# Holding large loads to about two under way, each tied to a TensorE instruction, with new places for all work

## The chip, the cores and the metric

The kernel runs on one core of a Trainium2 chip. The core has five engines with a program each: TensorE (PE in the profile, with its weight loads shown apart as PEld), VectorE (DVE), ScalarE (ACT), GpSimd (POOL) and SyncE (SP). Here SP starts nearly all transfers between memory and the core. They are carried out by 16 DMA engines, which also bring the engines' programs. The metric is the device time of one execution in microseconds, lower is better.

## The reference

Two layers are applied to x, a float32 array of 8 sequences x 512 rows x 256 features.

```python
# layer 1: an expert per sequence
h = gelu(x @ Wi[e] + bi[e])                 # 256 -> 1024, exact gelu
r = h @ Wo[e] + bo[e] + x                   # 1024 -> 256
x = layernorm(r) * gamma[e] + beta[e]
# layer 2: attention with 16 heads of 16, and a feed-forward part
emb = silu(sin_cos(timestep)) @ W_ada + b_ada
scale, shift = split(emb)
x = layernorm(x) * (1 + scale) + shift
scores = q @ k.T / 4 + attention_bias       # 8 x 16 x 512 x 512
scores = where(mask, -inf, scores)
x = x + softmax(scores) @ v @ Wo + bo
x = x + gelu2(layernorm(x) * g2 + beta2, W1, b1) @ W2 + b2    # 256 -> 1024 -> 256
```

The attention bias, called fside, is 134 MB of the 192 MB that are read. It is used once, element by element.

## The kernel before

All eight sequences pass through three kinds of work, which the kernel lets overlap. The expert layer and the projections to q, k and v (matmuls of 128x128 blocks; lines 689, 712, 863 and 911), the attention, and the feed-forward part (lines 689, 712 again, and 1052 for the last sequence).

The attention goes in steps. A step takes 32 query rows of one sequence with all 16 heads. There are 16 steps for a sequence, 128 in all. `attention_step` (L1097) makes a step's operations: a load of 1 MB of fside (`load_f`, L1112), one of the mask for four steps (L1118), the mask's conversion on GpSimd (L1124), the score matmuls into four banks (L1147; in one step of four the mask is added there by a matmul, L1140), in the other three steps the addition of the mask to fside on GpSimd (L1162, four instructions), the addition of scores and fside with the row maximum on VectorE (L1170, four instructions), the maximum's sign on GpSimd (L1183), the exponentials on ScalarE (L1191) and the transposes on VectorE (L1206). The score matmuls of the next step wait for the four additions at L1170, since these empty the banks. After four steps `attend` (L1216) multiplies the probabilities with v (L1246, 512 matmuls in four groups called sums0 to sums3), brings the row sums into place (L1262), divides, and multiplies with the output weights (L1289).

The buffer for fside has five tiles of two steps each (L354): a tile is free for a new load when the sums of its four steps are done.

The order of the work is set by a planner that runs while the program is built. The class `Weave` (L143) collects operations with an engine, a cost, a key and what they depend on. `run` (L180) then walks through a model of time. It keeps for each engine when it is free. Again and again it takes the operation that can start first, and among those that can start within 0.25 us of it, the one with the lowest key; it emits that operation. The order on each engine is therefore fixed when the program is built, and each engine carries out its own list in that order. On the chip an engine waits for another only through semaphores.

The keys come from tables. `PLACES` gives for each sequence where the stretches of the expert layer, the projections, the values and the feed-forward part begin and end, in units of attention steps, and how far other engines are ahead (`place`, L1075). `DUE` gives the lead of each kind of operation of a step, `LAST_DUE` the same for the last four steps, `AHEAD` how long before its first use a weight or an x buffer is loaded, and `PUT_BACK` how much an operation is put back in the choice when it needs another ScalarE table or another form of TensorE's tiles.

The planner also models how TensorE gets its program. A program is read in packets of 256 words (an instruction is a word; a matmul with its weight load makes two). Packet k is asked for when TensorE comes to word 155 + 256k, and the words from 192 + 256(k+1) on need it (`ASKED`, `NEEDED`). A packet is taken to land 2.4 us after whatever loads stand in the queue are done, and no sooner than 3.4 us after the request.

Because loads can stand before a packet, the planner keeps large loads (0.3 MB or more) away from requests. If fewer than 100 words are left to the next request (`NEAR`), a large load is put off by 4 us. After a request a large load may start only 0.4 us later (`CLEAR`). To hold the chip to that, `behind` (L1327) adds a dependence: each large load waits for one TensorE operation, the first that in the plan ends 0.4 us or more after the latest request. All large loads up to the next request share it. How many loads are under way at once has no limit of its own; the model knows only the time at which the queue is done (`queue`, L265).

## Time and profile before

| | us |
|---|---|
| median of 3 runs | 903.15 (903.09 to 904.28) |
| profiled execution | 905.54 |
| its span, first to last instruction | 903.8 |

| engine | busy us | share of the span |
|---|---|---|
| TensorE matmuls | 883.8 | 98% |
| GpSimd | 747.6 | 83% |
| VectorE | 736.4 | 81% |
| ScalarE | 691.8 | 77% |
| 16 DMA engines, data | | 58.5% |

The granted TensorE clock is full over the whole span (mean 1.000). In a row of the profile's groups or waits, L and a number give the line of the kernel, `out<-in` the tiles written and read, and `<-` before another engine's name tells who ended a wait. A row of waits gives the microseconds in total, how often, and the longest. A row of the time line gives the start, the busy time and the instruction, with the idle time before it in square brackets. "issue" stands for time in which the engine waited for nothing that the profile shows. A matmul's end is modelled, so that overlapping matmuls can look longer than their pace.

### The profile page before, as it was taken

To read this page: it belongs to the slowest core of one execution; us is meant where nothing else is said; L and a number is where in the kernel's file an instruction comes from. 1 tells how busy PE (TensorE), PEld (TensorE's weight loads), DVE (VectorE), ACT (ScalarE), POOL (GpSimd) and SP (SyncE) were. 2 spreads that over 40 slices of the span, in tenths; PEclk is the share of its full clock that TensorE was granted. 3 is DMA by queue.
4 is the path that set the end of the run, shared out by engine and by line. 5 is a ranking of instruction groups with operands and counts; after the bars stand their busy time and mean duration, and the time that the engine had idled before them with its cause. 6 is when DMAs were issued, how large, how long until landed. Compare 5 with 4: busy or idle time off the path is not lost.

```text
span 903.8 us, 31828 instructions
## 1 busy us (share of the span) xinstructions
PE 883.8 (98%) x13073; PEld 521.6 (58%) x13073; DVE 736.4 (81%) x1715; ACT 691.8 (77%) x1525; POOL 747.6 (83%) x844
## 2 busy tenths in 40 slices
PE   6999999999999999999999999999999899999998
PEld 2664564654664656545656456465465465465687
DVE  1216989998898978999978999899999889989930
ACT  3147979859959876797786995987977968989743
POOL 1189989999998996999799998999998899988720
PEclk9999999999999999999999999999999999999999
DMA  7697175475487466575575766485753666366230
GB/s 235 207 419 272 60 262 194 162 268 214 168 281 296 152 268 227 190 270 208 210 301 180 279 246 239 173 314 175 285 215 138 245 256 260 154 264 240 107 108 24
DMA packets 43160, 197.99 MB, mean 219 GB/s; under 512 B 4772, under 2 KB 12278, under 8 KB 24582
## 3 DMA queue, kind: packets, MB, share of 16 engines
q1 hardware_dynamic: 42724, 195.91, 58.5%
q8 instruction: 102, 1.67, 0.8%
q14 instruction: 44, 0.36, 0.1%
q10 hardware_dynamic: 290, 0.04, 0.0%
HBM read 191.73 MB, written 4.21 MB: 217 GB/s over the span
## 4 chain that ended last, share of the span: by engine, by line
PE 69%; POOL 17%; DMA 6%; issue 3%; ACT 3%; DVE 1%; SPq 0%; POOLq 0%; ACTq 0%; DVEq 0%
PE d L712 20%; PE d L689 15%; PE sc L1147 10%; PE d L1246 10%; POOL fs L1162 9%; PE d L863 4%; DMA fs<-in_fside_Bx16xSxS_dram 4%; POOL xn L764 4%; PE d L1289 2%; PE d L911 2%; PE d L1052 2%; ACT fs L1191 1%; DMA xn<-in_x_dram 1%; POOL mh L1124 1%; PE d L667 1%
## 5 line engine op out<-in xcount | busy, mean ns | idle before, releaser
L1162 POOL TENSOR_TENSOR fs<-fs,mh 128x512 f32<-128x512 f32 x384 | 436.3, 1163 | 26.9 <-DMA fs<-in_fside_Bx16xSxS_dram 16.5
L1191 ACT ACTIVATE fs<-fs,top 128x512 f32<-128x512 f32 x512 | 363.8, 714 | 87.7 <-POOL top L1183 87.1
L1170 DVE CUSTOM_DVE_ANT_0 fs<-sc,fs 128x512 f32<-128x512 f32 x512 | 326.4, 683 | 54.0 <-POOL fs L1162 21.5
L1206 DVE STREAM_TRANSPOSE fs<-fs 128x1024 f32<-128x1024 f32 x256 | 305.9, 1220 | 4.0 <-ACT fs L1191 3.9
L712 PE MATMUL d<-w,hid 128*128 128x256 f32 x1024 | 239.4, 384 | 0.0
L689 PE MATMUL d<-xt,w 128*128 128x512 f32 x480 | 225.7, 610 | 9.8 <-DMA w<-in_L_cond_Wi_dram 6.8
L712 PEld LDWEIGHTS d<-w,hid 128*128 128x128 f32 x1024 | 189.6, 190 | 56.2 <-issue 27.9
L689 PEld LDWEIGHTS d<-xt,w 128*128 128x128 f32 x480 | 87.6, 192 | 126.8 <-issue 100.5
L1147 PE MATMUL sc<-k,q 32*64 32x512 f32 x2048 | 146.4, 606 | 0.0
L1246 PEld LDWEIGHTS d<-fs,vb 64*32 64x32 f32 x8192 | 113.3, 105 | 42.7 <-issue 31.6
L1246 PE MATMUL d<-fs,vb 64*32 64x128 f32 x8192 | 132.4, 272 | 1.3 <-issue 1.2
L1191 ACT ACTIVATION_READ_ACCUMULATOR fs<-fs,top 128x1 f32 x512 | 97.5, 191 | 0.0
L1124 POOL TENSOR_SCALAR mh<-m 128x512 bf16<-128x512 uint8 x128 | 79.7, 623 | 10.4
L794 ACT ACTIVATE hid<-d,bc 128x512 f32<-128x512 f32 x64 | 41.7, 686 | 36.0 <-PE d L689 33.0
L1147 PEld LDWEIGHTS sc<-k,q 32*64 32x64 f32 x2048 | 35.3, 130 | 52.6 <-issue 22.3
L730 DVE BATCH_NORM_STATS2 st<-xn 128x6 f32<-128x256 f32 x96 | 40.2, 419 | 13.3 <-POOL xn L764 11.0
L1191 ACT ACT_TABLE_LOAD x38 | 48.8, 1283 | 0.7
L764 POOL TENSOR_TENSOR xn<-xn,bo 128x1024 f32<-128x1024 f32 x8 | 18.9, 2363 | 36.5 <-DMA xn<-in_x_dram 22.7
L1183 POOL TENSOR_SCALAR top<-top 128x4 f32<-128x4 f32 x128 | 25.3, 198 | 24.4 <-DVE top L1170 14.6
L1170 DVE DVE_READ_ACCUMULATOR2_ANT top<- 128x1 f32 x512 | 42.9, 84 | 0.0
L764 POOL TENSOR_TENSOR xn<-xn,rows 128x1024 f32<-128x1024 f32 x16 | 38.0, 2372 | 4.3 <-ACT xn L743 3.5
L986 ACT ACTIVATE hid<-d,col 128x512 f32<-128x512 f32 x56 | 35.8, 686 | 7.2 <-PE d L689 6.8
(100 smaller groups left out, 750.5 us busy)
## 6 DMA issues: line engine op xcount, KB each, us to landing
fs<-in_fside_Bx16xSxS_dram SPq DMA_DIRECT2D x128, 1024.0 KB
w<-in_L_cond_W_dram SPq DMA_DIRECT2D x16, 1024.0 KB
w<-in_L_cond_Wo_dram SPq DMA_DIRECT2D x8, 1024.0 KB
m<-in_mask_Bx1xSxS_bk_dram SPq DMA_DIRECT2D x32, 256.0 KB
w<-in_L_cond_Wi_dram SPq DMA_DIRECT2D x7, 1024.0 KB
xt<-in_x_turned_dram SPq DMA_DIRECT2D x8, 512.0 KB
xn<-in_x_dram SPq DMA_DIRECT2D x8, 512.0 KB
out_dram<-xn SPq DMA_DIRECT2D x32, 128.0 KB
```

The lines of the kernel that those rows point to most:

```text
L689: nc.tensor.matmul(h.tile, wt[:, c, f * P : (f + 1) * P], src.tile[:, c, :], start=(c == 0), stop=(c == ND - 1),)
L712: nc.tensor.matmul(h.tile[:, :D], lhs(f), wt[:, f, :], start=(f == 0), stop=(f == n - 1))
L730: nc.vector.bn_stats(st, src[:, t, :])
L764: lambda: nc.gpsimd.tensor_tensor(xn[b].tile, xn[b].tile, tiled(row()), alu),
L794: lambda: nc.scalar.activation(hid.tile[:, f, :], h.tile, AF.Gelu, bias=bc[b].tile[:, f : f + 1]),
L1124: nc.gpsimd.tensor_scalar(mh.tile, m8.tile[:, s % NI, :].bitcast(U8), MASKED, 1.0, ALU.mult, ALU.mult)
L1147: nc.tensor.matmul(banks[u][64 * r : 64 * r + 64, :], q_h[b].tile[quads[u], r, i, :], k_h[b].tile[quads[u], r, :], start=not joins, stop=True,
L1162: nc.gpsimd.tensor_tensor(f()[:, u, :], f()[:, u, :], mh.tile, ALU.add)
L1170: nc.vector.tensor_tensor_reduce(out=f()[:, u, :], in0=banks[u], in1=f()[:, u, :], scale=1.0, scalar=-3.0e38, op0=ALU.add, op1=ALU.max, ac ...
L1191: nc.scalar.activation(f()[:, u, :], f()[:, u, :], AF.Exp, bias=top.tile[:, u : u + 1], accum_out=den.tile[:, u, s % NI : s % NI + 1],)
L1206: nc.vector.transpose(two, two)
L1246: nc.tensor.matmul(pc[r].tile[QB * u : QB * u + QB, :P], vb_h[b].tile[half, j, u, :], t[half, :, :, u, QB * j : QB * j + QB], start=(j == ...
```

## The change

Three things change. First, a large load may now start in the plan only when at most 4.2 us of earlier transfers are left in the queue (`APART`); at 0.37 MB per us this is about one and a half loads of 1 MB. Second, the time kept clear after a request for a packet goes from 0.4 to 1.0 us (`CLEAR`). Third, the dependence that holds a large load back is chosen anew for each load: `recent` keeps the TensorE operations in order, and the load is tied to the latest of them that in the plan ends no more than 0.4 us after the load's own start. The old tie was to the end of the request's surroundings, which could lie far before the load.

With these rules all numbers of `PLACES`, `DUE`, `LAST_DUE`, `PUT_BACK` and `AHEAD` are replaced. So the order of the work on every engine is another. The operations, their sizes and their count are the same. No function is added.

```diff
 PLACES = {
     "up": [
-        (-43.62, -35.76, -9.79), (-10.08, -7.54, -8.47), (4.82, 6.37, 0.8), (16.16, 24.72, 3.59),
-        (40.19, 40.49, 9.26), (58.26, 59.96, 10.32), (74.13, 78.66, 0.43), (95.87, 102.96, 10.54),
+        (-39.19, -21.79, 3.06), (-14.61, 8.16, 5.64), (8.37, 8.24, 8.25), (15.42, 18.73, 6.65),
+        (38.6, 37.95, 0.46), (59.2, 60.13, 11.84), (72.75, 77.81, 2.08), (96.93, 99.72, 10.87),
     ],
...
 DUE = {
-    "load_m": -2.8, "load_f": 0.36, "convert": 5.45, "add": 3.5, "neg": 1.21, "exp": 7.79,
+    "load_m": 6.41, "load_f": 5.61, "convert": 6.13, "add": 4.66, "neg": -2.34, "exp": 8.15,
...
 AHEAD = {
-    "xt": 4.43, "wi": 5.3, "br": 21.51, "x": 1.61, "wo": 0.08, "row": 6.69, "w1": -5.35,
-    "w2": -4.96, "ss": 4.57, "bo": 9.01,
+    "xt": 5.82, "wi": 5.25, "br": 41.81, "x": -2.64, "wo": 0.97, "row": 9.79, "w1": 1.45,
+    "w2": 1.17, "ss": 3.05, "bo": 23.49,
 }
...
-    CLEAR = 0.4
+    CLEAR, APART = 1.0, 4.2
...
-        queue, clear, gate, landed = 0.0, -100.0, None, 0.0
+        queue, clear, landed, recent = 0.0, -100.0, 0.0, []
...
                             else:
                                 start = max(start, clear)
+                            start = max(start, queue - self.APART)
...
-                    clear, gate = at + self.CLEAR, None
+                    clear = at + self.CLEAR
...
-            if o.words and clear > 0.0 and (gate is None or gate[0] < clear):
-                gate = o.end, behind(None)
-            elif o.mb >= self.LARGE and gate is not None:
-                behind(gate[1])
+            if o.words and clear > 0.0:
+                recent.append((o.end, behind(None)))
+            elif o.mb >= self.LARGE and recent:
+
+                while len(recent) > 1 and recent[1][0] <= start + 0.4:
+                    recent.pop(0)
+                behind(recent[0][1])
```

More of the change, by code (lines that the diff above doesn't have):

```diff
@@ L59 @@
     "up": [
-        (-43.62, -35.76, -9.79), (-10.08, -7.54, -8.47), (4.82, 6.37, 0.8), (16.16, 24.72, 3.59),
-        (40.19, 40.49, 9.26), (58.26, 59.96, 10.32), (74.13, 78.66, 0.43), (95.87, 102.96, 10.54),
+        (-39.19, -21.79, 3.06), (-14.61, 8.16, 5.64), (8.37, 8.24, 8.25), (15.42, 18.73, 6.65),
+        (38.6, 37.95, 0.46), (59.2, 60.13, 11.84), (72.75, 77.81, 2.08), (96.93, 99.72, 10.87),
     ],
     "down": [
-        (-11.81, -10.05, 10.14), (-4.58, 13.95, 4.54), (8.87, 9.47, -5.98), (16.73, 19.65, -6.3),
@@ L65 @@
-        (40.46, 45.48, -3.47), (63.1, 67.19, -0.71), (69.95, 82.78, -4.3), (102.74, 103.99, 6.51),
+        (-20.03, -11.72, -7.86), (-7.71, 12.63, -2.49), (6.73, 11.61, 1.05), (14.3, 20.63, -5.29),
+        (42.99, 49.92, 0.54), (61.05, 71.22, 1.14), (72.07, 81.04, -5.39), (105.02, 107.12, 5.37),
     ],
     "norm": [
-        (9.71, -15.53, 14.76), (31.23, 198.14, 17.88), (46.96, 90.03, 27.3),
-        (-3.29, 172.59, -35.11), (64, -55.76, 7.58), (21.93, 53.72, -44.84),
-        (100.13, -120.62, 10.02), (103.92, -117.57, -1.06),
+        (1.44, -38.7, 8.38), (26, 230.24, 14.14), (38.85, 67.91, 18.14), (-5.46, 108.96, -35.61),
@@ L71 @@
+        (66.49, -96.63, 12.39), (5.81, 47.02, -58.5), (102.37, -144.13, 12.92),
+        (103.33, -191.46, -0.18),
     ],
     "project": [
-        (-2.64, -1.11, -9.92), (20.49, 12.69, 2.54), (23.07, 26.86, -1.46), (36.89, 63.96, 2.72),
-        (53.64, 66.71, -4.18), (76.36, 89.67, -0.98), (90.61, 100.48, 0.78),
-        (102.39, 116.12, -9.49),
+        (-6.24, 4.45, -1.69), (14.02, 6.13, 1.1), (19.71, 44.68, 0.79), (32.51, 62.55, -4.48),
+        (58.72, 68.47, 5.17), (66.86, 87.88, 1.49), (87.82, 106.61, -1.02),
@@ L76 @@
+        (100.6, 111.25, -10.23),
     ],
     "values": [
-        (3.57, 9.1, -1), (21.82, 33.22, 1.13), (39.61, 33.8, 3.49), (53.58, 70.14, -0.86),
-        (69.81, 68.46, 2.46), (82.31, 97.69, -0.8), (101.06, 90.65, -0.17),
-        (112.56, 112.45, 0.87),
+        (6.85, -2.11, 4.05), (23.34, 28.83, 2.2), (41.39, 46.26, 5.73), (52.7, 76.41, 5.22),
+        (64.67, 74.8, -3.7), (87.1, 85.66, -1.39), (106.54, 94.05, 0.4), (120.74, 117.22, 0.29),
     ],
     "last_norm": [
-        (25.14, 12.56, 0.32), (40.69, 48.12, -3.3), (62.39, 53.06, -5.43), (81.92, 87.74, 3.92),
@@ L84 @@
-        (84.13, 103.16, 3.07), (109.67, 129.5, -5.33), (118.65, 123.92, -5.19),
+        (31.46, 14.48, 3.22), (47.66, 48.8, 3.82), (62.37, 45.5, 0.03), (87.36, 82.07, 9.04),
+        (80.56, 86.1, -12.16), (102.32, 101.81, -14.17), (113.14, 142.82, 1.95),
     ],
     "last_up": [
-        (28.82, 25.08, 6.08), (35.47, 40.18, 0.67), (66.32, 52.95, -1.98), (74.48, 89.37, -4.47),
-        (98.9, 107.27, -9.13), (112.96, 117.07, 1.01), (125.16, 123.41, 3.62),
+        (28.21, 27.9, -1.53), (45.03, 36.84, 0.32), (63.3, 61.62, -8.49), (78.86, 86.69, 1.7),
@@ L89 @@
+        (106.21, 105.05, -5), (115.6, 120.99, 3.41), (126.4, 122.67, 0.57),
     ],
     "last_down": [
-        (27.06, 36.61, -3.94), (55.01, 42.07, -1.93), (75.63, 60.54, 4.28), (81.96, 95.18, 4.08),
-        (104.06, 119.74, 1.18), (117.15, 124.04, 0.23), (125.29, 136.74, -0.43),
+        (33.42, 41.59, 2.09), (56.4, 48.61, -3.15), (70.03, 73.09, 6.84), (82.44, 89.88, 0.1),
+        (109.79, 121.46, -1.54), (127.98, 122, -1.76), (125.8, 143.77, 3.59),
     ],
     "last_part": [
-        (131.41, 259.4, -0.64), (259.56, 321.86, -1.29), (274.57, 311.97, 7.81),
+        (139.14, 253.36, 1), (286.03, 296.98, 0.82), (276.89, 303.93, -3.06),
@@ L99 @@
 DUE = {
-    "load_m": -2.8, "load_f": 0.36, "convert": 5.45, "add": 3.5, "neg": 1.21, "exp": 7.79,
-    "turn": 9.78, "rec": 11.99, "diagonal": 7.14, "sums0": 5.77, "sums1": 2.88, "sums2": 10.44,
-    "sums3": 4.92, "own": 7.36, "spread": 9.56, "divide": 7.43, "out": 10.17, "out_add": 12.64,
-    "load_f2": -1.03, "masked": 0.44,
+    "load_m": 6.41, "load_f": 5.61, "convert": 6.13, "add": 4.66, "neg": -2.34, "exp": 8.15,
+    "turn": 9.92, "rec": 11.1, "diagonal": 9.03, "sums0": 5.15, "sums1": 2.58, "sums2": 9.05,
+    "sums3": 3.42, "own": 5.11, "spread": 13.61, "divide": 8.42, "out": 10.91, "out_add": 14.5,
+    "load_f2": 5.25, "masked": -2.07,
 }
 LAST_DUE = {
-    "exp": 10.3, "turn": 1.32, "neg": -5.97, "rec": 16.75, "diagonal": 19.97, "sums0": 9.5,
-    "sums1": 3.93, "sums2": 10.9, "sums3": 19.76, "own": 12.05, "spread": 47.46, "divide": 57.23,
-    "out": 72.84, "out_add": 79.8,
+    "exp": 1.08, "turn": 8.34, "neg": 2.72, "rec": 31.77, "diagonal": 30.22, "sums0": 10.64,
+    "sums1": 13.03, "sums2": 17.16, "sums3": 20.95, "own": 31.22, "spread": 23.21,
+    "divide": 49.04, "out": 87.17, "out_add": 79.99,
 }
 PUT_BACK = {
-    "table": 12.31, "tiles": 0.6,
+    "table": 12.27, "tiles": 0.84,
 }
 AHEAD = {
-    "xt": 4.43, "wi": 5.3, "br": 21.51, "x": 1.61, "wo": 0.08, "row": 6.69, "w1": -5.35,
-    "w2": -4.96, "ss": 4.57, "bo": 9.01,
+    "xt": 5.82, "wi": 5.25, "br": 41.81, "x": -2.64, "wo": 0.97, "row": 9.79, "w1": 1.45,
+    "w2": 1.17, "ss": 3.05, "bo": 23.49,
 }
```

## The prediction

> **What bounds the kernel now.** I read the busy shares first, then TensorE's groups and waits, then the time line around its longest pause, and last the waits of the load queue and of GpSimd.

> ```profile
> span 903.8 us, 31828 instructions
> PE 883.8 (98%) x13073; PEld 521.6 (58%) x13073; DVE 736.4 (81%) x1715; ACT 691.8 (77%) x1525; POOL 747.6 (83%) x844
> q1 hardware_dynamic: 42724, 195.91, 58.5%
> q8 instruction: 102, 1.67, 0.8%
> ```

> TensorE (PE) is busy for 883.8 of 903.8 us; every other engine has 156 us or more free, and the DMA engines are 58.5% used. Queue q8 carries TensorE's program: 102 packets of 16 KB. The 20.0 us in which TensorE shows no matmul fall in three parts: 6.8 us until its first weights land, 3.2 us after its last matmul (900.5 us), and 10.0 us between. TensorE's waits name most of those 10:

> ```profile
> PE d L689 <- DMA w<-in_L_cond_Wi_dram: 6.8, 1, 6.8
> PE sc L1140 <- DVE top L1170: 2.3, 2, 1.7
> PE sc L1140 <- POOL mh L1124: 1.4, 3, 1.0
> PE d L689 <- DVE vc L917: 1.2, 1, 1.2
> PE d L1246 <- issue: 1.2, 1, 1.2
> ```

> Only the last of these is a program fetch: nothing in the profile holds the matmul. The time line shows it in the middle of a group:

> ```profile
> 756.74 2.89 PE L1246 MATMUL d<-fs,vb 64*32 64x128 f32 x191
> 760.81 0.27 PE L1246 MATMUL d<-fs,vb 64*32 64x128 f32 x1 [1.18 <-issue]
> ```

> From the DMA packets of q8 I take packet 84: it landed at 759.42 and TensorE went on 1.39 us later, at its word 85x256+192. At packet 50 it is the same: landed 497.75, went on at 499.09 (+1.34), at word 51x256+193. So a packet is needed 293 words after it is asked for (the planner's 155 and 192 fit). Request to start of the packet is 1.18 us in the median of all 102, its transfer 1.0, and 1.39 more until it is usable: some 3.5 us. TensorE waits only where it runs 293 words in less, which are the short L1246 groups (about 2 us per 256 words).

> **The change part by part.**

> *Limit and tie of large loads.* Of 184 large loads the trace lets me follow 176: 53 were issued with none under way, 55 with one, 40 with two, 28 with three to five. 36 of the 102 packets began more than 1.6 us after the request, the worst 6.9 us (at 591 us, behind four loads). But that worst one stopped nothing: its slack was used up. Stops that fetches made are 1.44 us at 760.81 (its packet began 1.09 us after the request, so no load stood in its way) and 0.35 us at 499.09 (1.96 us, a load did). The price of loads in front of packets is thus 0.35 us of 903.8, and that is what the limit can give back directly.

> [...] I go by the rows: gain 0.35.

> *What is moved by the new places.* The built program has the same 6733 matmul instructions, but other neighbours. From the trace's times I priced 293-word stretches in its order: before has five below 3.45 us (2.57, 2.72, 3.02, 3.03, 3.27), after has one (2.01). That leaves one sure stop of 3.45 - 2.01 = 1.44 us, against 1.79 us measured before. With the above this is one term: **-0.4 us**, at most -1.2 (if all five cost their count, 2.6 against 1.4).

> *Tile changes of TensorE.* Going between full, score and sums forms happens 341 times before and 346 after. A price: the eight L712 matmuls are 1.99 us right after a score group and 1.89 otherwise.

> ```profile
> 598.64 1.99 PE L712 MATMUL d<-w,hid 128*128 128x256 f32 x8
> 600.48 1.03 PE L1289 MATMUL d<-wo_t,ctx 128*128 128x256 f32 x4
> 601.34 1.89 PE L712 MATMUL d<-w,hid 128*128 128x256 f32 x8
> 603.16 1.11 PE L1147 MATMUL sc<-k,q 32*64 32x512 f32 x16
> ```

> Five more at 0.10 is **+0.5 us**, all on the bound.

> *ScalarE tables.* 84 table loads in place of 79, 1283 ns each: +6.4 us on an engine that is 77% busy. It hides behind TensorE; ScalarE holds 3% of the chain that ended last, so 3% of 6.4, **+0.2**; without cover, 6.4.

> *Waits of the load queue (SP).* SP waits for TensorE 150 times in place of 80, in 258 semaphore instructions in place of 202. SP itself has time: 290 loads and stores, about 0.35 us each. What matters is what stands behind a waiting load in the same queue: the 32 mask loads, the 32 output stores that free x buffers, and the weights of the next layer; GpSimd L1162 and L1124 and TensorE L689 wait for these. Rows of before:

> ```profile
> SPq L1112 <- PE sc L1147: 125.7, 16, 16.1
> SPq L953 <- DVE xn L946: 115.8, 26, 13.0
> POOL fs L1162 <- DMA fs<-in_fside_Bx16xSxS_dram: 16.5, 15, 3.1
> ```

> I counted TensorE work between the instruction that an fside load is tied to and the score group that needs it. Median before 18.9 us, after 15.8; under 8 us stand 5 of 128 before, 13 after. Is 8 us enough? The quick loads land 4.5 us after issue, four mask additions at 1.16 us end at 9.1, the last maximum at 9.9; the next score group, which needs these banks, comes about 904/128 = 7.1 us after the first, at 15. So 5 us are spare, or 1 us with 4.2 us of other loads ahead. A limit by itself delays no landing as long as the DMA engines stay fed, since loads land in order anyway. So I take **0**. From both sides: the 3.7 us that L1140 waited before (its two rows) could double, +3.7, or half of it could go because a late-needed load no longer stands behind early ones, -1.9.

> *Start and end.* The first nine TensorE operations and the last forty stand in the same order in both: 0. The other 5 us of waits for other engines (10.0 - 1.2 - 3.7) are scattered chance meetings of an order; another order has its own, taken as equal, +/-2.

> **Sum**: -0.4 + 0.5 + 0.2 + 0 = +0.3 on a span of 903.8, so 904.1. The profiled execution took 905.54 (1.7 us around its span); the median of the runs is 903.15, and the shift put on that gives **903.4 us**. What a measurement of this kernel can tell from no change is about 0.2%, 1.8 us: 901.3 to 905.0.

> **The rivals.**
> *Late data (slower).* Loads lose their head start and GpSimd's 16.5 us of waiting for fside doubles, each pause passed on to the banks of the next score group. For it: 13 instead of 5 short distances, and in-order SP, where one tied load holds the masks. Against it: the 5 us spare. Price: L1140's 3.7 us doubled and another 1.5 us at the projections and weights, about +5: 908. It decides from the point where GpSimd waits over 25 us for fside.
> *Loads in the way mattered more (faster).* Needed loads wait behind early ones: at 121.0 us an fside load issued behind two others landed at 128.8, and GpSimd and then L1140 (1.7 us) paused. If half of the 8.8 us of waits for engines goes, and 1.2 of fetches: -5.6 + 0.7, 898.3. Against it: landing order is issue order, limit or not.
> *It does nothing.* The forecast itself nearly; the ties then show in SP's waits alone.

> **How the numbers follow.** No measurable change 0.37, with its own range 901.3 to 905.0; late data or an unlucky order 0.34; faster 0.29. Cases of both signs hold most of the chance, so the range runs to both: down by 3.7 + 0.5 to 899.2 and up by 3.7 + 1.1 to 908.2, beyond which I leave 1 in 10 on each side.

> **What would show it.** Packets starting over 1.6 us after the request should fall from 36 to under 20 with at most one fetch stop of 1 us or more; no large load should go out with three others under way; TensorE's busy time should stay within 2 us of 883.8; GpSimd's wait for fside should stay between 12 and 25 us. The prediction is wrong if TensorE's pauses between first and last matmul leave 7 to 14 us.

## The result: 916.8 us in place of 903.1

The changed kernel takes 916.79 us in the median (914.35 to 920.3), the kernel before 903.12 in the same job. The ratio is 1.016, with an interval of 1.0142 to 1.0179: 13.7 us more. The forecast was 903.4 with a range up to 908.2. It was wrong in size and in what it took for likeliest, and even its slower rival (908) was too mild.

The profiled execution took 920.3 us with a span of 918.5. These lines of its page answer to those shown of before. The rows by slices are busy shares and the granted clock in tenths.

```profile
span 918.5 us, 31865 instructions
PE 889.7 (97%) x13073; PEld 523.4 (57%) x13073; DVE 738.3 (80%) x1715; ACT 698.2 (76%) x1530; POOL 747.3 (81%) x844
PEclk9999999899999999999999999999999989999999
```

The span grew by 14.7 us. TensorE's idle time grew from 20.0 to 28.8 (+8.8), its busy time from 883.8 to 889.7 (+5.9). The busy time of the same 13073 matmuls should not grow. The third line says why it can: two of the forty slices show a clock below nine tenths, where before the mean clock was 1.000. After, it is 0.988. (The profiled execution is the slowest of the four of after; the other three show 0.992 to 0.994.) (All line numbers of after are three higher: L1246 is now L1249.)

TensorE's waits of after (microseconds in total, how often, the longest):

```profile
PE d L692 <- DMA w<-in_L_cond_Wi_dram: 6.9, 1, 6.9
PE d L1249 <- issue: 6.4, 3, 3.6
PE d L715 <- DMA w<-in_L_cond_W_dram: 3.3, 1, 3.3
PE sc L1143 <- DVE fs L1209: 3.0, 2, 2.7
PE d L627 <- DMA fs<-in_L_cond_W_ada_dram: 2.0, 1, 2.0
```

The first row is the start, as before. The row "issue" was 1.2 us and is 6.4: TensorE stood still with nothing to wait for but its program. A weight load comes 3.3 us late, another 2.0; neither row was there. The waits of L1140 for VectorE and GpSimd (3.7 us), which the forecast watched, have gone. The time line of TensorE shows the four pauses of over 2 us between the first 25 us and the end:

```profile
170.38 0.63 PE L1143 MATMUL sc<-mh,sel 32*64 32x512 bf16 x2 [2.72 <-DVE fs L1209]
170.39 2.33 PE L1150 MATMUL sc<-k,q 32*64 32x512 f32 x16
...
480.66 3.46 PE L715 MATMUL d<-w,hid 128*128 128x256 f32 x8 [3.28 <-DMA w<-in_L_cond_W_dram]
...
595.75 1.50 PE L1249 MATMUL d<-fs,vb 64*32 64x128 f32 x86 [2.09 <-issue]
...
744.17 1.06 PE L1249 MATMUL d<-fs,vb 64*32 64x128 f32 x19 [3.63 <-issue]
745.16 3.78 PE L866 MATMUL d<-xt,wq_t 128*128 128x512 f32 x4
```

The first, third and fourth are program fetches. From the packets of queue q8: packet 10 landed at 168.94 and TensorE went on 1.44 us later; packet 62 at 594.27 (+1.48); packet 80 at 742.70 (+1.47). That is the delay of 1.34 and 1.39 us of before. TensorE also goes on within two words of word 192 of a packet each time, where the prediction placed these stops. So the first pause, which the wait row puts down to VectorE, is a fetch as well; VectorE had only been the last engine to release something. The second pause is the weight w2.

Each pause is followed by slow matmuls: the eight L715 take 3.46 us where eight take 1.89 to 1.99 at full clock, the four L866 3.78 where four take 1.98. The windows of the trace around the four pauses have the stretch, its length, the busy time of TensorE, its weight loads, VectorE, ScalarE and GpSimd, then the granted clock, the DMA share and GB/s:

```profile
166.94:170.35 3.41, 0.72 (x34) 0.23 (x19) 2.91 (x5) 3.40 (x6) 2.98 (x6) 1.00 0.20 71
170.35:177.18 6.83, 6.80 (x43) 3.97 (x44) 4.18 (x11) 4.14 (x9) 5.33 (x6) 0.50 0.37 130
477.55:480.96 3.41, 0.30 (x2) 0.30 (x3) 3.34 (x10) 2.12 (x7) 3.17 (x5) 1.00 0.90 294
480.96:484.38 3.42, 3.42 (x16) 2.24 (x22) 0.60 (x1) 3.01 (x8) 1.49 (x4) 0.50 0.32 134
593.60:597.01 3.41, 1.32 (x94) 1.26 (x97) 3.41 (x7) 3.38 (x8) 3.25 (x5) 1.00 0.01 2
597.01:600.42 3.41, 3.41 (x54) 1.26 (x36) 2.07 (x4) 3.24 (x8) 3.25 (x3) 0.50 0.02 5
740.38:743.79 3.41, 0.16 (x11) 0.00 (x0) 3.37 (x6) 1.15 (x4) 2.93 (x7) 1.00 0.70 291
743.79:750.62 6.83, 6.45 (x39) 2.07 (x38) 0.00 (x0) 5.35 (x12) 3.99 (x5) 0.50 0.60 205
```

In each pair the first row holds the pause at full clock, the second runs at half: 6.83 + 3.42 + 3.41 + 6.83 = 20.5 us. At half clock a busy TensorE loses half of that, 10.2 us. Row by row against full-clock durations I get 3.3 at 170, 1.6 at 481, 1.6 at 597 and 3.3 at 744, 9.8 us. In the other three executions the mean clocks of 0.992 to 0.994 give an estimate of 5 to 7 us for the same loss, so its size differs from execution to execution.

The start looks like half clock too, in both kernels. The time line of before and then of after:

```profile
6.82 6.57 PE L689 MATMUL d<-xt,w 128*128 128x512 f32 x8 [6.82 <-DMA w<-in_L_cond_Wi_dram]
...
13.48 10.57 PE L689 MATMUL d<-xt,w 128*128 128x512 f32 x24
```

```profile
6.88 5.18 PE L692 MATMUL d<-xt,w 128*128 128x512 f32 x8 [6.88 <-DMA w<-in_L_cond_Wi_dram]
```

Before, the first eight matmuls take 0.82 us each, the next 24 of the same shape 0.44. The trace's record of the clock begins only at 12.66 us before, and at 9.93 after, in both with full clock; the matmuls ahead of that are slow. So the mean of 1.000 leaves out the start, and after's eight, 1.4 us faster, are luck: they had the full clock earlier.

With that the 14.7 us can be set out. I count a stop of TensorE as a fetch where it goes on at word 192 of a packet's 256, or one or two words behind it, 1.2 to 1.6 us after that packet landed. Before has one such stop, after eight.

| TensorE, us | before | after | change |
|---|---|---|---|
| fetch stops | 1.2 | 10.8 | +9.6 |
| waits for the weights w2 and W_ada | 0 | 5.3 | +5.3 |
| other waits between first and last matmul | 8.7 | 2.5 | -6.2 |
| before the first and after the last matmul | 10.2 | 10.2 | +0.1 |
| half clock behind the four pauses | 0 | 9.8 | +9.8 |
| half clock at the start (estimated: half the time to the first record) | 2.9 | 1.5 | -1.4 |
| busy time that is shorter elsewhere | | | -2.5 |

The last row is what is left over; I can't put it down to a cause. The third row matters for the rivals: the new order does have fewer waits for other engines.

### The profile page after: what moved, and what is told of

The parts are those of the page before. It is cut to its first block, busy times and chain, and to the rows that moved or that the text cites. A ratio compares the mean times of both kernels' runs of the same rounds, so it can differ in the third digit from the quotient of the medians.

```text
span 918.5 us, 31865 instructions
## 1 busy us (share of the span) xinstructions
PE 889.7 (97%) x13073; PEld 523.4 (57%) x13073; DVE 738.3 (80%) x1715; ACT 698.2 (76%) x1530; POOL 747.3 (81%) x844
## 3 DMA queue, kind: packets, MB, share of 16 engines
q1 hardware_dynamic: 42724, 195.91, 58.0%
q8 instruction: 102, 1.67, 0.7%
## 4 chain that ended last, share of the span: by engine, by line
PE 78%; POOL 11%; DMA 3%; issue 3%; ACT 3%; DVE 2%; SPq 0%; POOLq 0%; DVEq 0%; ACTq 0%
PE d L715 22%; PE d L692 17%; PE d L1249 12%; PE sc L1150 12%; POOL fs L1165 6%; PE d L866 5%; POOL xn L767 3%; PE d L1292 3%; PE d L914 2%; PE d L1055 2%; PE d L670 1%; PE sc L1143 1%; POOL mh L1127 1%; PE d L1265 1%; DMA w<-in_L_cond_W_dram 1%
## 5 line engine op out<-in xcount | busy, mean ns | idle before, releaser
L1165 POOL TENSOR_TENSOR fs<-fs,mh 128x512 f32<-128x512 f32 x384 | 435.8, 1163 | 31.2 <-DMA fs<-in_fside_Bx16xSxS_dram 21.4
L1173 DVE CUSTOM_DVE_ANT_0 fs<-sc,fs 128x512 f32<-128x512 f32 x512 | 326.3, 683 | 58.5 <-POOL fs L1165 18.8
L715 PE MATMUL d<-w,hid 128*128 128x256 f32 x1024 | 242.3, 388 | 3.8 <-DMA w<-in_L_cond_W_dram 3.3
L715 PEld LDWEIGHTS d<-w,hid 128*128 128x128 f32 x1024 | 191.9, 192 | 65.1 <-issue 32.5
L1249 PEld LDWEIGHTS d<-fs,vb 64*32 64x32 f32 x8192 | 113.6, 105 | 49.7 <-issue 39.2
L1249 PE MATMUL d<-fs,vb 64*32 64x128 f32 x8192 | 133.8, 272 | 6.5 <-issue 6.4
L1194 ACT ACT_TABLE_LOAD x40 | 51.3, 1283 | 0.7
L767 POOL TENSOR_TENSOR xn<-xn,bo 128x1024 f32<-128x1024 f32 x8 | 18.9, 2363 | 38.7 <-DMA xn<-in_x_dram 23.2
L1186 POOL TENSOR_SCALAR top<-top 128x4 f32<-128x4 f32 x128 | 25.3, 197 | 28.4 <-DVE top L1173 16.1
L1230 POOL TENSOR_TENSOR dg<-cst,den 128x512 f32<-128x512 f32 x32 | 34.1, 1066 | 9.5 <-DVE den L1225 8.5
L767 POOL TENSOR_TENSOR xn<-xn,ss 128x1024 f32<-128x1024 f32 x16 | 37.9, 2371 | 3.5 <-ACT xn L746 2.7
```

The lines of the kernel that those rows point to most:

```text
L715: nc.tensor.matmul(h.tile[:, :D], lhs(f), wt[:, f, :], start=(f == 0), stop=(f == n - 1))
L767: lambda: nc.gpsimd.tensor_tensor(xn[b].tile, xn[b].tile, tiled(row()), alu),
L1165: nc.gpsimd.tensor_tensor(f()[:, u, :], f()[:, u, :], mh.tile, ALU.add)
L1173: nc.vector.tensor_tensor_reduce(out=f()[:, u, :], in0=banks[u], in1=f()[:, u, :], scale=1.0, scalar=-3.0e38, op0=ALU.add, op1=ALU.max, ac ...
L1194: nc.scalar.activation(f()[:, u, :], f()[:, u, :], AF.Exp, bias=top.tile[:, u : u + 1], accum_out=den.tile[:, u, s % NI : s % NI + 1],)
L1249: nc.tensor.matmul(pc[r].tile[QB * u : QB * u + QB, :P], vb_h[b].tile[half, j, u, :], t[half, :, :, u, QB * j : QB * j + QB], start=(j == ...
```

## The experiments

Each kernel ran beside the kernel before on the same chip. From chip to chip the kernel before took 901.9 to 904.0 us, so that the ratios compare better than the times. The ratios of those that change only the ties or the order stand in this table; "order" is the order that the places, the limit and the clear time give together, since no one of these can be changed without moving the rest.

| large loads tied | order of before | order of after |
|---|---|---|
| as in before (old tie) | 1 | 1.0219 (1.0186 to 1.0251) |
| as in after (new tie) | 1.0049 (1.0031 to 1.0067) | 1.0160 (1.0142 to 1.0179) |
| not at all | 1.0048 (1.0024 to 1.0073) | 1.0143 (1.0099 to 1.0187) |
| only fside, each order with its own tie | 1.0043 (1.0028 to 1.0059) | 1.0150 (1.0110 to 1.0190) |

Read across, the order of after costs 0.95% to 2.2% with any tie. Read down, the old tie is the best in the old order and by its median the worst in the new, where the intervals of the other three overlap.

### The order of after with the old tie

```diff
-            if o.words and clear > 0.0:
-                recent.append((o.end, behind(None)))
-            elif o.mb >= self.LARGE and recent:
...
+            if o.words and clear > 0.0 and (gate is None or gate[0] < clear):
+                gate = o.end, behind(None)
+            elif o.mb >= self.LARGE and gate is not None:
+                behind(gate[1])
```

> The changed kernel with the old tie alone put back; the order on every engine stays that of the changed kernel. Theory (the new ties let loads out just ahead of packet requests, and the long pauses of TensorE that follow also halve its clock): the pauses at 168 and 741 us shrink below 1.5 us, no stretch at half clock follows them, and the time falls from 916.8 to 903-909 us. Rival (the new order by itself is worse, the ties are innocent): 914-919 us, with the same long pauses.

It took 924.19 us, 1.0219. That the new tie is the guilty part falls: in this order it saves some 5 us against the old one by the ratios. Fetches stop TensorE for 10.3 us in seven places, the longest 3.1 us, with the pause at 171 us (2.5 us) among them, and the clock is halved for 17 us in three stretches.

### The order of before with the new tie

```diff
...
-            elif o.mb >= self.LARGE and gate is not None:
-                behind(gate[1])
+            elif o.mb >= self.LARGE and recent:
...
+                while len(recent) > 1 and recent[1][0] <= start + 0.4:
+                    recent.pop(0)
+                behind(recent[0][1])
```

> The kernel before with the new tie alone; places and order are those of before, no limit on loads under way. Theory (ties are guilty): packets that start over 1.6 us after their request rise from 36 to 50 or so, pauses over 2 us appear, 908-916 us. Rival (the order is guilty): 902-905 us, packets as before.

It took 908.33 us, 1.0049. 49 packets start more than 1.6 us after the request, in place of 36. In the profiled execution the clock stays full; its longest pauses are 1.4 and 1.9 us, so the pauses over 2 us that the theory named did not come. The new tie costs 4.3 us in the old order.

### No tie at all, in either order

The lines from `if o.words and clear > 0.0` to the last `behind` that make the ties are left out: seven in the kernel of after, four in that of before.

> The order of the changed kernel with no tie on any large load: each load goes out as soon as SP reaches it and its tile is free. The old tie gave a ratio of 1.022 in this order, the new one 1.016. If a tie of any kind costs by holding loads, no tie gives 0.995 to 1.010 (899 to 912). If the order itself makes the close packets and the tie only chooses which loads meet them, no tie gives 1.015 to 1.030 (917 to 930), with at least three pauses over 2 us and 10 to 27 us of half clock.

> The kernel before with no tie on any large load, the order unchanged. If the old tie keeps packets free of loads in this order, leaving it out gives 1.005 to 1.02 (908 to 921) and over 36 packets that start more than 1.6 us after the request. If that order bears any tie, because few of its packets follow close on another, it gives 0.998 to 1.005 and no stretch of half clock.

In the new order 914.68 us, in the old 908.02. So the ties of after are worth nothing that can be measured in their own order (916.79 and 914.68, with overlapping intervals), and the old tie is worth 4 us in the old one. The expectation of over 36 late packets in the old order came true with 51, and there are two stretches of half clock; the ratio of 1.0048 is at the lowest end of what was expected. In the new order the direction of the second case came true, but not its figures: 1.0143 is below 1.015, two pauses are over 2 us (4.18 and 2.26) and not three, and there is one window of half clock, 3.4 us. That is the execution that was profiled, of 912.5 us and a mean clock of 0.998. The slowest of the four took 920.1 us at 0.991. Without ties fetches stop TensorE for 14.5 us in thirteen places, and no wait for a weight is left after the start.

### The order of before, only fside loads tied

```diff
             elif o.mb >= self.LARGE and gate is not None:
-                behind(gate[1])
+                if o.emit.__name__ == "load_f":
+                    behind(gate[1])
```

> The kernel before with its old tie on the 128 fside loads alone; weights and x buffers go free. If a tied weight load delays work, 0.994 to 0.999 (898 to 902), with fewer waits of TensorE for weights. If weights in front of packets matter as much as fside does, 1.001 to 1.01 (904 to 912). Being even faster than the kernel before would make it the best of the kernels that do all the work.

906.87 us, 1.0043, not faster. It shows what one load does. The time line of SP, before first, then this kernel, and then TensorE's in this kernel:

```profile
758.82 0.34 SPq L557 DMA_DIRECT2D w<-in_L_cond_W_dram  x1
```

```profile
752.11 0.38 SPq L558 DMA_DIRECT2D w<-in_L_cond_W_dram  x1
```

```profile
753.74 1.21 PE L1247 MATMUL d<-fs,vb 64*32 64x128 f32 x69
759.13 0.27 PE L1247 MATMUL d<-fs,vb 64*32 64x128 f32 x1 [4.19 <-issue]
759.33 0.66 PE L668 MATMUL d<-ident,hn 128*128 128x128 f32 x4
759.92 1.96 PE L1247 MATMUL d<-fs,vb 64*32 64x128 f32 x64
```

The last of these rows has this one for its counterpart in the kernel before:

```profile
761.60 1.16 PE L1246 MATMUL d<-fs,vb 64*32 64x128 f32 x64
```

This is packet 84, the one stop of the kernel before. Tied, the weight went out at 758.82, after the packet had started (758.46, 1.09 us after its request), and the pause was 1.18 us. Untied, the weight goes out at 752.11, 0.6 us ahead of the request at 752.70. The packet starts 4.03 us after the request, the pause is 4.19 us, and then 64 of the L1247 take 1.96 us where 64 took 1.16: a window at half clock follows. Two stores of output go out ahead of the weight in both kernels. One load in front of one packet costs 3.0 us of fetch and about 1.7 us of clock.

### After, with loads tied past the request word

Every load whose tie lies between words 130 and 204 of a packet is tied to the first TensorE operation past word 204, where the load's first reader leaves room.

```diff
+        for load, n, o in ties:
+            m = n
+            while m + 1 < len(words_at) and (words_at[m][1] - self.FROM) % 256 < self.UPTO - self.FROM:
+                m += 1
...
+            behind(words_at[m][0], load)
```

> The changed kernel, same order, but every large load whose tie falls between word 130 and word 204 of a packet's 256 is tied to the next TensorE operation past word 204 instead (where its first reader leaves room). Theory (the request comes nearer to word 192 than to 155, so that loads let out there stand before the packet): the packet pauses at 168 and 741 us go, the pause for the weight at 477 us stays, 904-911 us. Rival (order is guilty, or later loads starve GpSimd): 914 us or more.

977.93 us, 1.0821, the worst of all. In TensorE's waits fetches hold 14.3 us in the first row alone, and work that came late takes more:

```profile
PE d L1259 <- issue: 14.3, 12, 3.5
PE d L1302 <- DVE ctx L1292: 9.1, 2, 8.6
PE d L680 <- POOL xn L777: 7.3, 2, 4.8
```

In after, a wait of SP of 11.4 us at one load held the weight that stood behind it in SP's list (below); I take it that the loads held longer here do the same to what stands behind them, though no row shown here follows one. The clock is halved for 37 us. The edit is too coarse to say more than that.

### Only fside loads tied, in after

```diff
-                behind(recent[0][1])
+                if o.emit.__name__ == "load_f":
+                    behind(recent[0][1])
```

> The changed kernel with the tie kept for the fside loads alone; weights, x and rows are free of it. Theory (the limit and the tie made the weight at 480 us late): that pause of 3.3 us shrinks below 2, its stretch at half clock goes, 910-914 us. Rival (the place in SP's order makes it late, the tie costs nothing): 915-919 us with the same pause.

915.9 us, 1.0150: no change beyond the uncertainty. The time is that of the rival, the pause that of the theory. The weight at 480.66 of after now comes 2 us less late, and the time line shows the same eight matmuls at full clock:

```profile
477.79 1.97 PE L716 MATMUL d<-w,hid 128*128 128x256 f32 x8 [1.30 <-DMA w<-in_L_cond_W_dram]
...
740.29 1.06 PE L1250 MATMUL d<-fs,vb 64*32 64x128 f32 x19 [3.36 <-issue]
```

1.97 us in place of 3.46: the pause of 1.30 us is not followed by half clock, that of 3.28 us was. What was won there was lost elsewhere: a fetch stop of 0.35 us in after is now one of 2.27 us (at 666), and the untied weights make 57 late packets in place of 52.

### Pauses of known length, in before

In the kernel before, seven TensorE instructions wait for a chain of ScalarE copies, so that pauses of growing length come at places without other trouble.

```diff
+    PAUSES = {4: 4, 13: 6, 17: 8, 23: 10, 30: 12, 36: 14, 40: 18}
...
+    def pause(n):
+        last = nc.cur_bb.bb.instructions[-1]
+        for k in range(n):
+            nc.scalar.copy(still, still)
+            if k == 0:
+                depend(nc.cur_bb.bb.instructions[-1], last)
+        return nc.cur_bb.bb.instructions[-1]
```

> The kernel before with seven pauses put into TensorE's first 75 us: after seven of its operations 4, 6, 8, 10, 12, 14 and 18 small ScalarE copies (on a tile of their own) must end before the next operation, about 1 to 5 us each, some 20 us in all. Theory (a pause of over about 2 us is followed by 3.4 or 6.8 us at half clock): the pauses of 1 to 1.7 us cost their own length, those over 2.4 us are each followed by a stretch at 0.5 of the clock, 928-938 us. Rival (the half clock in the changed kernel has another cause, such as load on the chip): no stretch at 0.5 follows them, 918-924 us.

The pauses of 1.22 and 1.77 us are not followed by half clock; those of 2.32, 2.87, 3.83, 3.98 and 5.08 us are, each for one stretch of 3.4 us. The time line at the second and third, and the windows around the third:

```profile
33.79 7.17 PE L720 MATMUL d<-w,hid 128*128 128x256 f32 x32 [1.77 <-ACT still L1358]
43.29 5.34 PE L720 MATMUL d<-w,hid 128*128 128x256 f32 x16 [2.32 <-ACT still L1358]
```

```profile
39.77:43.18 3.41, 1.20 (x6) 0.72 (x4) 1.03 (x3) 1.90 (x8) 0.54 (x1) 1.00 0.57 189
43.18:46.60 3.42, 3.31 (x8) 2.69 (x9) 0.00 (x0) 0.06 (x1) 1.81 (x1) 0.50 0.72 274
```

After 1.77 us of pause 32 matmuls take 7.17 us, 0.22 each. After 2.32 us 16 take 5.34, 0.33 each: 3.6 us at their former pace, so 1.7 us is the price of the half clock. Nothing else was changed at either place. (The kernel's time, 938.18 us in one execution, holds the pauses themselves.)

### Three fside loads cut to a quarter, in after

```diff
+FEW = (17, 106, 107)
...
-            nc.sync.dma_start(f(), fside[b, i].rearrange("h q u k -> (h q) u k"))
+            some = S // 4 if loads[0] in FEW else S
+            loads[0] += 1
+            nc.sync.dma_start(
+                f()[:, :, :some], fside[b, i].rearrange("h q u k -> (h q) u k")[:, :, :some]
+            )
```

> The changed kernel with three of its 128 fside loads cut to a quarter of their columns: the one that goes out at 162.6 us and the two at 736.1 and 736.5 us (their other columns keep what the buffer held; that part of the attention is left out). Theory A (these loads stand before TensorE's packets, and the pause is long enough to halve the clock): the pauses at 168 and 741 us fall from 2.7 and 3.6 us to below 1.5, the two stretches of 6.8 us at half clock go, 905-909 us. Theory B (packets are too close to each other in the new order, loads or not): the pauses stay above 2 us, 914-918 us.

909.91 us, 1.0079: three of the 128 loads are worth 6.9 us. The pauses shrink, but not below 1.5 us, and the time is 0.9 us above the range of theory A. In the time line the pause at 170 falls from 2.72 to 1.95, that at 744 from 3.63 to 1.71 (packets 10 and 80):

```profile
168.73 0.40 PE L1152 MATMUL sc<-mh,sel 32*64 32x512 bf16 x2 [1.95 <-issue]
...
739.24 0.62 PE L1258 MATMUL d<-fs,vb 64*32 64x128 f32 x19 [1.71 <-issue]
739.79 1.98 PE L871 MATMUL d<-xt,wq_t 128*128 128x512 f32 x4
```

The four L871 after the second are at full clock again. At 168.7 one window of half clock is left, in place of two. Saved are 0.8 + 1.9 us of pauses and 10.2 us of half clock in these two places, of which about half is time: 7.8, against 6.9 in all; the half clock at 597 is gone as well (a pause of 1.79 us there), and the weight's pause got two windows of it in place of one.

### All later fside loads cut to a quarter, in after and in before

The same edit with loads 12 to 127.

> The changed kernel with all fside loads from the thirteenth on cut to a quarter of their columns (the rest of those scores is left out); order, waits and ties stay. Theory A (loads in front of packets): packet pauses above 2 us go, at most one stretch at half clock stays, 899-906 us. Theory B (the order alone brings the packets too close, or engines wait for each other): pauses above 2 us stay, 910 us or more.

> The kernel before with the same cut of fside loads from the thirteenth on. Theory A (before, loads cost TensorE little): 899-903 us, and the packet pause at 760 us stays, since no load stood in its way. Rival (loads in the way cost several us before the change too): below 898 us.

After so cut takes 907.28 us (1.0056), before so cut 898.45 (0.9958). Both fall between the two cases that were expected. By the ratios the full size of the fside loads costs after some 9.4 us and before some 3.8. But 8.8 us of difference remain between the orders with little fside traffic: about two thirds of the loss is not the full size of these loads. The traces account for it: TensorE is idle between its first and last matmul for 13.1 us against 7.0, and has 6.8 us of half clock against none, which is 3.4 us of time. The largest pauses are that for the weight (3.2 us) and a fetch stop of 2.2 us at packet 62, each with a window of half clock behind it; two more fetch stops are of 1.4 and 1.0 us. The one fetch stop of before stays (1.6 us).

Packet 62 had loads in front of it as well, but small ones. SP's time line in after:

```profile
590.12 0.35 SPq L497 DMA_DIRECT2D rows<-in_L_cond_gamma_dram  x1
590.56 0.38 SPq L1121 DMA_DIRECT2D m<-in_mask_Bx1xSxS_bk_dram  x1
```

These are 0.25 MB each, less than the 0.3 MB from which the planner's rules hold. They go out 1.1 and 0.65 us ahead of the request at 591.2. In the four executions where they do so (after, its two kernels with cut loads, and the one with held loads) packet 62 starts 2.0 to 2.3 us after its request and stops TensorE for 1.95 to 2.15 us. In the same order with the old tie and with none, no load goes out in the 6 us ahead; it starts 0.95 and 1.05 us after the request, and the stop is 0.9 and 1.0 us. So half of this stop too is loads in the way.

### After, with the three loads held instead of cut

All the work is done here. Loads 17, 106 and 107 are only tied to TensorE operations that need the packet they stood in front of.

```diff
+    LATER = {17: 5, 106: 3, 107: 3}
...
+                for held in later:
+                    held[0] -= 1
+                    if not held[0]:
+                        behind(recent[-1][1], held[1])
```

> The changed kernel, all its work done, the order of every engine unchanged; only the ties of fside loads 17, 106 and 107 are moved to TensorE operations that need the packet which these loads stood in front of (they go out at about 172 and 745 us in place of 162.6 and 736.1). If loads in front of packets that follow close on another, and the half clock after the pauses, cost what is thought, the pause at 170 falls from 2.72 to under 2 and that at 744 from 3.63 to under 2, both half-clock stretches there go or shrink, and the time falls by 4 to 8 us: 908 to 913, ratio 1.006 to 1.011, as with the three loads cut to a quarter. If it was the smaller amount of data in that run and not its place in front of the packets, the time stays at 915 to 919. If the held loads come late for the mask additions, GpSimd's wait for fside grows by over 5 us and the time stays above 915 too.

921.57 us, 1.0202 (1.0175 to 1.0228): by the median slower than after, though the two intervals just touch, and certainly no gain, although both pauses went as expected. The time line at the two places, then at a new one:

```profile
166.97 0.40 PE L1153 MATMUL sc<-mh,sel 32*64 32x512 bf16 x2 [1.27 <-DVE fs L1219]
...
743.68 0.62 PE L1259 MATMUL d<-fs,vb 64*32 64x128 f32 x19 [0.89 <-issue]
744.24 1.99 PE L876 MATMUL d<-xt,wq_t 128*128 128x512 f32 x4
...
753.04 0.63 PE L680 MATMUL d<-ident,hn 128*128 128x128 f32 x4 [2.54 <-DVE xn L1308]
```

Packet 10 started 2.5 us after packet 9 had landed, in place of 4.2. The half clock at both places is gone. In return GpSimd's wait for fside rose from 21.4 to 28.1 us, TensorE waits 2.5 us for VectorE at 753, 1.5 us at 212, and 4.4 us for the weight at 482. These pauses halve the clock for 17 us. The mechanism at each packet is confirmed; that it can be had for nothing by holding these loads so is refuted. The third case of the expectation, late data, is what came.

## Why the prediction was wrong

**"The price of loads in front of packets is thus 0.35 us."** This step failed. It read the price from the stops that were left. But those were few because the old tie prevented the others: with no tie in the same order the time rises by 4.3 us, and with only the weights untied one load in front of one packet makes a stop of 1.18 us into one of 4.19. The trace of before did show 6.9 us of delay for a packet; I wrote it off because that packet had slack. The right question was how many packets have none.

**"Before has five stretches below 3.45 us, after has one."** This step failed too. It counted each stretch of 293 words alone. In the traces no packet starts while another is on its way: among 1414 packets of 14 executions none starts less than 2.1 us after the one before has landed (the shortest is 2.32 us in before and 2.36 in after). Where the request comes in flight or less than 0.5 us after the landing, and no data moves, the packet starts about 1.8 us or more after the request. Where it comes 1 to 2.5 us after the landing, also with no data moving, the start is mostly 0.6 to 1.7 us after the request. Requests while the last packet was still in flight: about 10 of 101 before, 15 after. Packets 9 and 10 are such a pair: 10 was asked for at 163.05, 9 landed at 163.71, and load 17 had gone out at 162.62; 10 started at 167.86. Fetch stops were to fall from 1.8 to 1.4 us; they are 10.8, of which 6.4 + 2.7 = 9.1 stand in the row "issue" and in the pause at 170. The one stop that I had counted, of 1.44 us, came at packet 62 with 2.09, and was of about 1 us where no small load stood in front.

**The limit and the tie, "0".** The ratios agree in part: leaving the tie of after out changes nothing measurable. But the step "A limit by itself delays no landing as long as the DMA engines stay fed" missed the weights, since the engines did not stay fed. (Its other half, that loads land in the order of issue, is what the two in front of packet 10 show: the pieces of load 17 end at 167.18, those of the mask load issued 0.42 us later at 167.86.) From 467.5 to 472.8 us no data moved in after, while SP waited at the load of an x buffer:

```profile
SPq L456 <- PE d L692: 11.4, 1, 11.4
```

W2 stood behind it in SP's list. It went out at 472.98, 1.1 us behind the x buffer (0.7 of that its own tie), landed 7.5 us after its issue and stopped TensorE for 3.3 us. With weights and x buffers untied SP still waits 11.4 us at this place, so that wait is not the tie's; W2 then goes out 0.4 us behind the x buffer, and the pause is 1.3 us. W_ada stopped TensorE for 2.0 us at 25; the cause of that is open. The L1140 waits of 3.7 us, for which I had set the bounds, went to nearly nothing outside the fetch at 170.

**What the sum lacked: the clock.** Before shows a mean clock of 1.000, so I gave it no term, and missed the slow matmuls at the start of the same trace. By rows it came to 9.8 us, as much as the fetch stops; in the other executions it is estimated at 5 to 7. By the inserted pauses, at 1.7 us for a window and one or two windows, a pause of 3 us costs not 3 us but an estimated 4.7 to 6.4. The four pauses of after, of 2.09 to 3.63 us, all have half clock behind them; of the inserted ones those of 2.32 us and more have it, those of 1.22 and 1.77 us have not.

**The rivals.** "Late data" had the sign, but the data that came late were weights (5.3 us, where it had put 1.5 at projections and weights together) and not fside: GpSimd's wait for fside is 21.4 us, below the 25 from which that case was to decide. Late fside came only in the kernel with the three loads held. "Loads in the way" was right that waits for other engines would fall (by 6.2 us, where it had 4.4); but the new order put loads in the way of packets, and the fetch stops took more than that back.

**The signs named.** Packets that start over 1.6 us after the request: under 20 expected, 52 measured, wrong. At most one fetch stop of 1 us: three, wrong. No load issued with three under way: nearly so, 6 of the 179 large loads that the trace of after lets me follow, where the same count gives 36 in before. TensorE's busy time within 2 us: +5.9, wrong. GpSimd's wait for fside 12 to 25 us: 21.4, right. Pauses between first and last matmul 7 to 14 us: 28.8 - 6.9 - 3.3 = 18.6, wrong. The 84 ScalarE table loads and SP's waits came as counted from the program; what they and the five tile changes cost no run tells apart.

**What stays open.** The limit, the clear time and the places were not separated. Packet 80 is late beyond what loads explain: with loads 106 and 107 held it still started 5.3 us after the word that I take for its request, with no data on the DMA engines. I don't know at which word a request is truly made in the dense stretches. No kernel here that does all the work beats the one before. The half clock of the executions that were not profiled is known only by its mean.

## What to carry to other kernels

A rare stall in a tuned kernel doesn't measure what its safeguards are worth: take the safeguard away, or count the places with no slack, before pricing it. When the order changes, list pairs of requests that come closer than one fetch (here 3.5 us), and ask which load, small ones included, goes out just ahead of the second. And price any pause of TensorE of about 2 us or more with the half clock after it: about 1.7 us for each window, as measured here behind the inserted pause of 2.32 us.

## What was new about the hardware

On such a grid it matters how a pause lies. The order of after without ties has one of 2.26 us with no half clock behind it. Its time line and windows:

```profile
368.52 1.78 PE L708 MATMUL d<-w,hid 128*128 128x256 f32 x7 [2.26 <-issue]
```

```profile
363.56:366.97 3.41, 2.70 (x147) 2.10 (x145) 3.20 (x9) 1.12 (x5) 3.04 (x6) 1.00 0.80 320
366.97:370.38 3.41, 1.86 (x9) 1.66 (x10) 0.78 (x3) 3.41 (x8) 2.39 (x4) 1.00 0.92 315
370.38:373.79 3.41, 3.41 (x35) 2.04 (x34) 3.17 (x8) 1.76 (x6) 1.82 (x2) 1.00 0.43 120
```

The edge at 366.97 cuts the pause into 0.71 and 1.55 us, and neither window was followed by half clock.

**Two packets waited for about the whole of a load that went out just ahead of them.** Packet 84 of before started 1.09 us after its request with no load ahead, and 4.03 us with one weight load of 1 MB ahead: 2.9 us more. At the 294 GB/s of the window at 477.55 a load of 1 MB takes an estimated 3.6 us. In that execution the last 8 KB piece of the load ends at 756.72, and packet 84 starts at 756.72. Packet 10 of after started 4.2 us after packet 9 had landed, with load 17 and a mask load of 0.25 MB in front, and 2.5 us without them. There the data of the two loads end at 167.86, and the packet starts at 167.86.

The trace has a 1 MB load as 128 pieces of 8 KB, an estimated eight for each of 16 engines. Neither of the two packets started between the pieces; why, no run here shows.
